# A decoder layer on one core: the second group's expert blocks placed between the first group's, their loads issued earlier, and the last norms on ScalarE

## The chip, the cores and the metric

The kernel runs on one NeuronCore of a Trainium2 chip. The metric is the device time of one execution in microseconds. Time before: 1847.62 us, the median of three runs (1845.48 to 1850.51).

## The reference

A post-norm decoder layer on x of 16 sequences x 256 tokens x 256 channels, all in float32:

```python
x = layernorm(x + attention(x))          # 16 heads, mixes the batch
x = layernorm(x + cross_attention(x, ctx))  # two softmaxes, one subtracted with a gain
x = layernorm(x + ffn(x))                # four experts, the best two of each token
```

The change lies in the last line. The router gives each token logits over four experts; the two best are weighted by a softmax over their two logits. The experts, each from 256 channels to 256:

```python
e0 = silu(x @ sw_w1) * (x @ sw_w3) @ sw_w2                       # "first", 1024 wide
e1 = gelu(((x @ me_eq_w + ..) @ me_wv + ..) @ me_wo .. @ me_c1w + ..) @ me_c2w + ..   # "second", 512 wide
h2 = layer_norm(syn + attn); h2 = layer_norm(h2 + relu(h2 @ ce_f1w + ..) @ ce_f2w + ..)
e2 = h2 @ ce_gen_w + ce_gen_b                                    # "third"
e3 = gelu(x @ ml_w1 + ml_b1) @ ml_w2 + ml_b2                     # "fourth", 1024 wide
out = layernorm(x + rw0 * e[sel0] + rw1 * e[sel1])
```

Constant matrices that follow each other (those of e1, and syn and attn of e2) are multiplied together early in the kernel, so second has one wide product `mw` and third one product `xw` in their place.

## The kernel before

**Tiling.** The 4096 tokens are 32 chunks of 128, four chunks to a pair (512 tokens), eight pairs. The sum x lies in SBUF all the time as `xs`. The two attentions run over the pairs. Each pair, as its cross-attention ends, is routed (`routing`), and its rows are written by GpSimd's indirect DMA into a list in DRAM with one stretch for each expert (`listing`, L404). There are two lists: group 0 holds the tokens of pairs 0 to 6, group 1 those of the last pair. Once the lists are written, each list's lengths are read into registers (`known`), and all later expert work stands under branches on them: a block of an expert has four chunks (512 tokens), and `block` does four chunks, two, or none, by the length.

**A block.** `load` brings 512 list rows into an `xe` buffer (three of them) from SP's queue; `turn` transposes them on TensorE into `xeT` (two buffers), the upper half copied from PSUM by ScalarE, the lower by VectorE (L478). `wide` multiplies with a wide weight into one PSUM bank (8 banks in turn), ScalarE applies GELU, SiLU or ReLU into `hid`; `product` multiplies back to 256 channels, VectorE writes the result into `ye` (one buffer; L504, L506), and SP writes it over the same list rows (L507). `first` comes in two parts (wide, back), `third` in three (product and norm; turn, wide and back product, norm; turn and last product); they are generators, so that the caller places the parts.

**The order.** The instruction order of TensorE, ScalarE and VectorE is the order in which the program writes them down; SP's and GpSimd's queues are laid out by the compiler's scheduler. [...]In the attentions a planner with due times places the work; in the last steps of the cross-attention, at fixed step numbers, `begin` issues the first loads of second in group 0 and `early` places four of its blocks. `turn_tokens` (L1404) turns each finished pair's tokens for the router; for the last two pairs it does so in the `ye` buffer. When the attentions have ended, six weights of the experts are loaded (`sw_w1` to `ml_w2`, L1585), and `rest` does what remains:

1. second's blocks 4 and 5 of group 0, with the first loads of third and first;
2. a loop over third and first of group 0, their parts alternating;
3. fourth's four blocks of group 0; meanwhile `gathers(0)` fetches each token's first expert row from the list by indirect DMA (L628, four for a pair, two slots `ya`), and `add` multiplies it by its weight and adds it to `xs` (L638);
4. group 1: second, third, first and fourth, and between their parts `both`: `add` of the second expert row of one or two pairs and `end`, the layer norm of the pair on VectorE (L140 to L147) and its output DMA.

Blocks beyond the expected lengths (`beyond`) stand under branches that this data does not take.

Of the kernel before, what the change touches and what calls it, by code (L numbers as in the profile page):

```python
# [15 lines left out]
P = 128  # L16
# [54 lines left out]
def decoder_kernel(ctx: ExitStack, tc: tile.TileContext, a: dict, out: bass.AP):  # L71
# [350 lines left out]
    class Experts:  # L422
# [3 lines left out]
        def __init__(self, fe, wb, mw, mb):  # L426
            self.wb, self.mw, self.mb, self.turns = wb, mw, mb, 0
            self.count, self.loaded, self.ready, self.done = {}, [], [], 0
            self.rings = {}
            self.ring(fe, "xe", 3, [P, CPB, D])  # L430
            self.ring(fe, "xeT", 2, [P, 2, TB])
            self.ring(fe, "ye", 1, [P, CPB, D])
            self.ring(fe, "hid1", 1, [P, 4, TB])
# [14 lines left out]
        def known(self, g):  # L448
            self.count[g] = [
                nc.values_load(moe["count"][0:1, g, e:e + 1], min_val=0, max_val=SIZES[g]) for e in range(5)  # L450
            ]
# [14 lines left out]
        def load(self, g, e, i, x=None):  # L466
# [3 lines left out]
            self.loaded.append(x)  # L470

        def turned(self, src, n, t):

            for c in range(2):
# [3 lines left out]
                (DVE.tensor_copy if c else ACT.copy)(t[:, c, :n * P], pt[:, :n * P])  # L478

        def turn(self):  # L480
            t = self.next("xeT")
            self.turned(self.loaded.pop(0), CPB, t)
            self.ready.append(t)
# [25 lines left out]
        def second(self, g, i, sure=False):  # L509
            xT, y, r = self.ready.pop(0), self.next("ye"), self.row(g, 1, i)  # L510
# [11 lines left out]
        def first(self, g, i):  # L522

            xT, r = self.ready.pop(0), self.row(g, 0, i)
# [15 lines left out]
        def fourth(self, g, i, sure=False):  # L540
            xT, y, r = self.ready.pop(0), self.next("ye"), self.row(g, 3, i)
# [11 lines left out]
        def third(self, g, i):  # L553

            xT, r = self.ready.pop(0), self.row(g, 2, i)
# [54 lines left out]
        def begin(self):  # L610
            self.load(0, 1, 0)
            self.load(0, 1, 1)
            self.known(0)
            self.turn()

        def early(self):
            i = self.done
            self.load(0, 1, i + 2)
            self.turn()
            self.second(0, i)  # L620
            self.done += 1


        def gather(self, q, k):
            self.slot = (self.slot + 1) % 2
            t = self.ya[:, self.slot]
# [7 lines left out]
        def add(self):  # L634
            q, k, t = self.gathered.pop(0)
            for n in range(CPB):
                x = xs[:, q * CPB + n, :]
                DVE.scalar_tensor_tensor(x, t[:, n, :], moe["weight"][:, q * CPB + n, k:k + 1], x, ALU.mult, ALU.add)  # L638

        def end(self, q):  # L640
            x = xs[:, q * CPB:(q + 1) * CPB, :]
            layernorm(tiny, x, x)
            SP.dma_start(out=out_v[:, q * CPB:(q + 1) * CPB, :], in_=x)

        def beyond(self, e, i0, i1, work):

            held = self.loaded, self.ready, {k: list(v) for k, v in self.rings.items()}
            with ExitStack() as levels:
                for i in range(i0, i1):
                    levels.enter_context(tc.If(self.count[0][e] > 4 * P * i))  # L650
                    self.loaded, self.ready = [], []
                    self.rings = {k: list(v) for k, v in held[2].items()}
                    self.load(0, e, i)
                    self.turn()
                    work(0, i, True)
            self.loaded, self.ready, self.rings = held

        def rest(self, fl, xw, xb, rb):
# [5 lines left out]
            self.load(0, 2, 0)  # L664
            self.turn()
            self.second(0, 4)
            self.load(0, 0, 0)
            self.turn()
            self.second(0, 5)
            x3 = self.wb.tile([P, CPB, D], F32, tag="cx", name="x3")  # L670
            self.beyond(1, 6, n, self.second)


            with ExitStack() as levels:
                for i in range(n):
                    levels.enter_context(tc.If(self.count[0][4] > 4 * P * i))
                    self.turn()
                    b, c = self.third(0, i), None
                    next(b)
                    if i + 1 < n:  # L680
                        self.load(0, 2, i + 1)
                        self.load(0, 0, i + 1)
                    c = self.first(0, i)
                    next(c)
                    next(b)
                    if i + 1 < n:
                        self.turn()
                    next(c)
                    next(b)
            assert not self.loaded and not self.ready  # L690


            self.ya = self.wb.tile([P, 2, CPB, D], F32, tag="cxp", name="ya")
            self.slot, self.gathered = 0, []
            self.load(0, 3, 0, x3)
            self.load(0, 3, 1)
            self.turn()
            pairs = iter(range(NPAIR - 1))

            def gathers(k, most=2):  # L700
                for q in range(most):
# [4 lines left out]
            gathers(0)  # L706
            ahead = [(0, 3, 2), (0, 3, 3), (1, 1, 0), (1, 2, 0)]
            for i in range(4):
                self.load(*ahead[i])
                if i < 3:  # L710
                    self.turn()
                self.fourth(0, i)
                while self.gathered:
                    self.add()
                gathers(0)
            self.beyond(3, 4, n, self.fourth)
            while self.gathered:
                self.add()


            pairs = iter(range(NPAIR - 1))
            self.known(1)
            gathers(1)
            self.turn()

            def both():
                for q, k, t in list(self.gathered):
                    self.add()
                    if q < NPAIR - 1:
                        self.end(q)  # L730
                gathers(1)

            self.load(1, 0, 0)
            self.turn()
            self.second(1, 0)
            both()
            b = self.third(1, 0)
            self.load(1, 3, 0)
# [851 lines left out]
```

## Time and profile before

| | |
|---|---|
| median of the runs | 1847.62 us |
| profiled execution | 1848.87 us, its span 1846.9 us |
| TensorE busy | 1682.0 us (91%) |
| VectorE busy | 960.4 us (52%) |
| ScalarE busy | 942.6 us (51%) |
| GpSimd busy | 536.5 us (29%) |
| mean granted TensorE clock | 0.958 |
| experts begin (first transposed block) | at 1291.3 us |
| loop over third and first | 1407.7 to 1579.9 us |
| fourth's blocks of group 0 | 1589.6 to 1705.4 us |
| group 1 and the ends | 1705.4 to 1846.9 us; TensorE busy 79 us of it |

The span runs from the first to the last instruction; the execution's own time is some 2 us more. A line of a timeline gives the start, the duration, the engine and line of the kernel, the operation with output and inputs, and in brackets the idle time of the engine before it and what ended that. L119 is the helper of all products, so its rows are told apart by their tiles: `pw` is a wide product, `pr` a product back to 256 channels, `pt` a transposed block. A busy engine is counted by its instructions' durations; waits are not busy.

### The profile page before, as it was taken

To read this page: it belongs to the slowest core of one execution; us is meant where nothing else is said; L and a number is where in the kernel's file an instruction comes from. 1 tells how busy PE (TensorE), PEld (TensorE's weight loads), DVE (VectorE), ACT (ScalarE), POOL (GpSimd) and SP (SyncE) were. 2 spreads that over 40 slices of the span, in tenths; PEclk is the share of its full clock that TensorE was granted. 3 is DMA by queue.
4 is the path that set the end of the run, shared out by engine and by line. 5 is a ranking of instruction groups with operands and counts; after the bars stand their busy time and mean duration, and the time that the engine had idled before them with its cause. 6 is when DMAs were issued, how large, how long until landed. Compare 5 with 4: busy or idle time off the path is not lost. (4 is left out here: it accounts for less than half of the span.)

```text
span 1846.9 us, 32370 instructions
## 1 busy us (share of the span) xinstructions
PE 1682.0 (91%) x12254; PEld 960.4 (52%) x12254; DVE 960.4 (52%) x2033; ACT 942.6 (51%) x1368; POOL 536.5 (29%) x1235
## 2 busy tenths in 40 slices
PE   6999999999999999999999999997987999899743
PEld 2343434343444656656565655564664758566533
DVE  1225656655556876777766666672213334121565
ACT  3547777777777576665655556554322222231210
POOL 5001313212313333344634343445320110131331
PEclk9999999999999999999999999898998999899876
DMA  9912111212112200000101000011333001221322
GB/s 258 297 50 70 65 59 59 69 59 93 58 59 98 65 14 14 3 25 14 37 2 36 2 25 2 25 37 47 102 103 109 20 28 48 82 75 39 106 64 81
DMA packets 117771, 115.34 MB, mean 62 GB/s; under 512 B 7776, under 2 KB 111408, under 8 KB 117584
## 3 DMA queue, kind: packets, MB, share of 16 engines
q1 hardware_dynamic: 108560, 93.08, 15.8%
q0 software_dynamic: 7824, 19.65, 3.6%
q8 instruction: 114, 1.87, 0.4%
q14 instruction: 73, 0.60, 0.1%
q10 hardware_dynamic: 1200, 0.15, 0.1%
HBM read 73.79 MB, written 38.54 MB: 61 GB/s over the span
## 5 line engine op out<-in xcount | busy, mean ns | idle before, releaser
L1307 DVE TENSOR_REDUCE mpad<-p 128x4 f32<-128x1024 f32 x256 | 311.3, 1218 | 142.3 <-PE p L119 141.4
L1313 ACT ACTIVATE e<-p 128x512 f32<-128x512 f32 x512 | 276.7, 596 | 175.5 <-PE p L119 173.7
L841 ACT ACTIVATE h<-ph,L_attn_b 128x1024 f32<-128x1024 f32 x256 | 271.3, 1112 | 160.9 <-PE ph L119 160.9
L119 PE MATMUL p<-qp,kT 32*128 32x256 f32 x2048 | 315.3, 410 | 18.2 <-DVE o L1360 13.3
L119 PE MATMUL p<-kT,qp 32*128 32x256 f32 x2048 | 314.1, 409 | 1.5 <-DVE mpad L1307 1.5
L119 PEld LDWEIGHTS p<-kT,qp 32*128 32x128 f32 x2048 | 193.7, 188 | 91.0 <-issue 49.7
L119 PEld LDWEIGHTS p<-qp,kT 32*128 32x128 f32 x2048 | 207.9, 190 | 31.7 <-issue 25.6
L119 PE MATMUL ph<-qT,w1p 32*128 32x512 f32 x1024 | 152.3, 652 | 3.1 <-ACT h L841 1.8
L935 DVE TENSOR_TENSOR z<-rqb,ra 128x1024 f32<-128x1024 f32 x120 | 151.5, 1265 | 3.7 <-DMA rqb<-rqd 1.7
L119 PE MATMUL pe<-h,w2p 128*32 128x512 f32 x1024 | 138.2, 612 | 1.6 <-DVE enc L858 0.9
L119 PE MATMUL pob<-e,vaug 128*32 128x512 f32 x1024 | 128.3, 620 | 0.0
L942 ACT ACTIVATE z<-z 128x1024 f32<-128x1024 f32 x120 | 127.1, 1060 | 1.3 <-DVE z L935 0.9
L628 POOL DMA_INDIRECT ya<-xlist,place x64 | 62.8, 981 | 205.0 <-DVE xs L638 86.7
L159 POOL TENSOR_SCALAR ln_ve<-ln_mv 128x2 f32<-128x2 f32 x32 | 7.2, 225 | 351.3 <-DVE ln_mv L157 350.5
L119 PE MATMUL pw<-xeT,L_ffn_sw_w 128*128 128x512 f32 (+1 forms) x256 | 85.8, 496 | 12.8 <-DVE xeT L478 12.8
L163 POOL TENSOR_SCALAR xs<-xs,ln_mv,rs_y 128x256 f32<-128x256 f32 x64 | 83.8, 1314 | 3.4
L478 ACT ACT_TABLE_LOAD x17 | 21.8, 1283 | 113.7 <-PE pt L477 113.3
L119 PE MATMUL po<-z,vaug 128*32 128x256 f32 x1024 | 72.8, 389 | 6.7 <-DVE ra L895 1.6
L119 PEld LDWEIGHTS pw<-xeT,L_ffn_sw_w 128*128 128x128 f32 x256 | 50.0, 196 | 47.1 <-issue 28.7
L404 POOL DMA_INDIRECT xlist<-xs,place x64 | 62.7, 980 | 37.1 <-DVE place L401 19.7
L119 PEld LDWEIGHTS ph<-qT,w1p 32*128 32x128 f32 x1024 | 42.5, 184 | 53.8 <-issue 42.0
L1339 ACT COPY ovTb<-pob 128x512 f32<-128x512 f32 x64 | 37.5, 585 | 58.2 <-PE pob L119 58.2
(349 smaller groups left out, 2598.1 us busy)
## 6 DMA issues: line engine op xcount, KB each, us to landing
rqb<-rqd SPq DMA_DIRECT2D x64, 512.0 KB
xlist<-zero SPq DMA_DIRECT2D x16, 1024.0 KB
xe<-xlist SPq DMA_DIRECT2D x21, 512.0 KB
xlist<-ye SPq DMA_DIRECT2D x14, 512.0 KB
xs<-in_x SPq DMA_DIRECT2D x8, 512.0 KB
cx<-in_ctx SPq DMA_DIRECT2D x8, 512.0 KB
qp<-st SPq DMA_DIRECT2D x256, 2.0 KB
out<-xs SPq DMA_DIRECT2D x8, 512.0 KB
```

What stands on the lines that cost most here:

```text
L119: PE.matmul(out=out_, lhsT=lhsT, rhs=rhs, start=start, stop=stop)
L159: POOL.tensor_scalar(ve, mv[:, :, 1], EPS, None, ALU.add)
L163: POOL.tensor_scalar(x, x, mv[:, i, 0:1], r[:, i:i + 1], ALU.subtract, ALU.mult)
L404: put = POOL.indirect_dma_start(xlist[g][:], bass.IndirectOffsetOnAxis(ap=place[:, n, k:k + 1], axis=0), xs[:, q * CPB + n, :], None)
L478: (DVE.tensor_copy if c else ACT.copy)(t[:, c, :n * P], pt[:, :n * P])
L628: POOL.indirect_dma_start(t[:, n, :], None, xlist[group(q)][:], bass.IndirectOffsetOnAxis(ap=moe["place"][:, q * CPB + n, k:k + 1], axis=0),)
L841: ACT.activation(h, phs[gp], AF.Tanh, bias=b1[:, fc:fc + 1])
L935: DVE.tensor_tensor(z, bc(rqbs[u][:, 2 * gp:2 * gp + 2], 2, 2), bc(rk, 3, S), ALU.mult)
L942: ACT.activation(z, z, AF.Exp)
L1307: DVE.tensor_reduce(mpads[j % 2][:, 2 * gp:2 * gp + 2, :, ic], p1, AX.X, ALU.max, negate=True)
L1313: ACT.activation(e[:, gi], p2[gi], AF.Exp)
L1339: ACT.copy(o, po)
```

## The change

It reorders the expert phase. Second's group 0 begins two steps later and its first block three; `turn_tokens` uses `x3`, a buffer now taken at the start, instead of `ye`; `ahead` issues the first loads of third and first before the weights' loads in the program; fourth's first two blocks are loaded before the loop in the program, into `x3` and a slot of `ya`; of group 1, third's three parts and first's two are placed between and after fourth's blocks of group 0; group 1's second and fourth come last, among the ends. A pair's end now does sum and statistics of a chunk in turn, computes the bias `nb` = -mean x r on VectorE and scales and shifts with ScalarE's Identity. The gathers of the second choice have a third slot, `x3`.

```diff
-            if t == 4 * (len(units) + LAG) + 2:
+            if t == 4 * (len(units) + LAG) + 4:
                 ex.begin()
-            if t - 4 * (len(units) + LAG) in (3, 12, 19, 27):
+            if t - 4 * (len(units) + LAG) in (6, 12, 19, 27):
                 ex.early()
         assert planA.ended() and planB.ended()
+        ex.ahead()
...
-                    xTs[q] = late[1].next("ye").rearrange("p c d -> p (c d)").rearrange("p (c t) -> p c t", c=2)
+                    xTs[q] = late[1].x3.rearrange("p c d -> p (c d)").rearrange("p (c t) -> p c t", c=2)
...
+        def ahead(self):
+
+            self.loaded += [self.load(0, 2, 0), self.load(0, 0, 0)]
...
-        def add(self):
+        def add(self, st=None):
             q, k, t = self.gathered.pop(0)
             for n in range(CPB):
                 x = xs[:, q * CPB + n, :]
                 DVE.scalar_tensor_tensor(x, t[:, n, :], moe["weight"][:, q * CPB + n, k:k + 1], x, ALU.mult, ALU.add)
-
-        def end(self, q):
-            x = xs[:, q * CPB:(q + 1) * CPB, :]
-            layernorm(tiny, x, x)
-            SP.dma_start(out=out_v[:, q * CPB:(q + 1) * CPB, :], in_=x)
+                if st is not None:
+                    DVE.bn_stats(st[:, n, :], x)
+            return q
+
+        def end(self):
+
+            st = tiny.tile([P, CPB, 6], F32, tag="ln_st", name="ln_st")
+            mv = tiny.tile([P, CPB, 2], F32, tag="ln_mv", name="ln_mv")
+            q = self.add(st)
+            for c in range(CPB):
+                DVE.bn_aggr(mv[:, c, :], st[:, c, :])
+            ve = tiny.tile([P, CPB], F32, tag="ln_ve", name="ln_ve")
+            DVE.tensor_scalar(ve, mv[:, :, 1], EPS, None, ALU.add)
+            r = rsqrt(tiny, ve, CPB)
+            nb = self.wb.tile([P, 2, CPB], F32, tag="rf", name="ln_nb")[:, 0, :]
+            DVE.scalar_tensor_tensor(nb, mv[:, :, 0], -1.0, r, ALU.mult, ALU.mult)
+            for c in range(CPB):
+                x = xs[:, q * CPB + c, :]
+                ACT.activation(x, x, AF.Identity, bias=nb[:, c:c + 1], scale=r[:, c:c + 1])
+            SP.dma_start(out=out_v[:, q * CPB:(q + 1) * CPB, :], in_=xs[:, q * CPB:(q + 1) * CPB, :])
...
-            self.load(0, 2, 0)
-            self.turn()
-            self.second(0, 4)
-            self.load(0, 0, 0)
-            self.turn()
-            self.second(0, 5)
-            x3 = self.wb.tile([P, CPB, D], F32, tag="cx", name="x3")
+            t5 = self.turn(self.loaded.pop(0))
+            self.second(0, 4, self.ready.pop(0))
+            b_ = self.turn(self.loaded.pop(0))
+            self.second(0, 5, t5)
             self.beyond(1, 6, n, self.second)
 
+            ya = self.wb.tile([P, 2, CPB, D], F32, tag="cxp", name="ya")
+            self.slots, self.gathered = [ya[:, 0], ya[:, 1]], []
+            a_, x0, x1 = self.loaded.pop(0), self.load(0, 3, 0, self.x3), self.load(0, 3, 1, ya[:, 1])
...
-            gathers(0)
-            ahead = [(0, 3, 2), (0, 3, 3), (1, 1, 0), (1, 2, 0)]
-            for i in range(4):
-                self.load(*ahead[i])
-                if i < 3:
-                    self.turn()
-                self.fourth(0, i)
-                while self.gathered:
-                    self.add()
-                gathers(0)
+            self.known(1)
+            x2, y2, x3 = self.load(0, 3, 2), self.load(1, 2, 0), self.load(0, 3, 3)
+            ta, tb = self.rings["xeT"]
+            self.turn(x0, ta)
+            self.turn(x1, tb)
+            gathers(0)
+            self.fourth(0, 0, ta)
+            adds()
+            gathers(0)
+            b = self.third(1, 0, self.turn(y2, ta))
+            next(b)
+            self.turn(x2, ta)
+            y0, y1 = self.load(1, 0, 0), self.load(1, 1, 0)
+            self.fourth(0, 1, tb)
+            adds()
+            gathers(0)
+            next(b)
+            self.turn(x3, tb)
+            y3 = self.load(1, 3, 0)
+            self.fourth(0, 2, ta)
+            adds()
+            gathers(0)
+            next(b)
+            c = self.first(1, 0, self.turn(y0, ta))
+            next(c)
+            self.fourth(0, 3, tb)
+            next(c)
+            adds()
+            self.turn(y1, ta)
+            self.rings["xeT"] = [tb]
             self.beyond(3, 4, n, self.fourth)
...
-            def both():
-                for q, k, t in list(self.gathered):
-                    self.add()
-                    if q < NPAIR - 1:
-                        self.end(q)
-                gathers(1)
-
-            self.load(1, 0, 0)
-            self.turn()
-            self.second(1, 0)
-            both()
-            b = self.third(1, 0)
-            self.load(1, 3, 0)
-            self.turn()
-            next(b)
-            c = self.first(1, 0)
-            next(c)
-            both()
-            next(b)
-            self.turn()
-            next(c)
-            both()
-            next(b)
-            self.gather(NPAIR - 1, 0)
-            self.fourth(1, 0)
-            both()
-            self.gather(NPAIR - 1, 1)
-            both()
-            self.end(NPAIR - 1)
+            self.slots.append(self.x3)
+            last = NPAIR - 1
+            pairs = iter(range(last))
+            gathers(1, 3)
+            self.end()
+            gathers(1, 1)
+            self.second(1, 0, ta)
+            self.turn(y3, tb, copies=(ACT.copy, ACT.copy))
+            self.end()
+            self.gather(last, 0)
+            self.end()
+            gathers(1, 1)
+            self.fourth(1, 0, tb)
+            self.end()
+            gathers(1, 1)
+            self.add()
+            gathers(1, 1)
+            self.end()
+            self.gather(last, 1)
+            for _ in range(3):
+                self.end()
```

The rest of the diff passes the turned block to `first`, `second`, `third` and `fourth` as an argument instead of through a list, and lets `beyond` load into `x3`.

## The prediction

> **What bounds the kernel now.** I read the engine totals first (TensorE is busy 1682.0 of 1846.9 us, everything else about half or less), then TensorE's own timeline of the last stage for the holes and what ended them, then VectorE's, ScalarE's and GpSimd's timelines where a hole ends on them. TensorE's timeline from 1268 us to 1400 us:
>
> ```profile
> 1291.33 1.97 PE L477 MATMUL pt<-ident,xe 128*128 128x128 f32 x8 [7.75 <-DMA xe<-xlist]
> 1350.12 3.64 PE L119 MATMUL pl<-xw,ye 128*128 128x4 f32 x16 [5.11 <-ACT ye L1414]
> 1353.62 1.95 PE L477 MATMUL pt<-ident,xe 128*128 128x128 f32 x8
> ...
> 1397.72 1.94 PE L477 MATMUL pt<-ident,xe 128*128 128x128 f32 x8 [11.84 <-DMA xe<-xlist]
> ```
>
> Columns are start, duration, engine, line, operation, shapes, count, and in brackets the idle time before it with its releaser. Three holes, 24.7 us, two of them waits for a load of list rows. The same view after 1540 us:
>
> ```profile
> 1583.97 1.06 PE L477 MATMUL pt<-ident,x 128*128 128x128 f32 x8 [4.03 <-DVEq L674]
> 1589.62 1.94 PE L477 MATMUL pt<-ident,xe 128*128 128x128 f32 x8 [4.58 <-DMA xe<-xlist]
> 1591.35 15.83 PE L119 MATMUL pw<-xeT,L_ffn_ml_w 128*128 128x512 f32 x32
> ...
> 1691.41 13.98 PE L119 MATMUL pr<-L_ffn_ml_w,hid 128*128 128x256 f32 x64
> 1707.59 3.39 PE L477 MATMUL pt<-ident,xe 128*128 128x128 f32 x16 [2.20 <-DVEq L648]
> ...
> 1740.97 15.83 PE L119 MATMUL pw<-xeT,L_ffn_sw_w 128*128 128x256 f32 x62 [12.84 <-DVE xeT L478]
> ...
> 1775.24 5.40 PE L119 MATMUL pw<-h2T,L_ffn_ce_f1w 128*128 128x256 f32 x14 [16.26 <-DVE h2T L478]
> ```
>
> From 1591 to 1705 us the fourth expert's blocks run without a hole. After 1705.4 TensorE is busy 79 of the remaining 141 us: the second group's experts alternate with VectorE's final sums and norms. One such final sum and norm on VectorE (its timeline, before the last pair):
>
> ```profile
> 1825.93 1.66 DVE L638 SCALAR_TENSOR_TENSOR xs<-ya,weight,xs 128x256 f32<-128x256 f32 x4
> 1827.52 1.40 DVE L140 BATCH_NORM_STATS2 ln_st<-xs 128x6 f32<-128x256 f32 x4
> 1828.83 0.36 DVE L142 BATCH_NORM_AGGREGATE ln_mv<-ln_st 128x2 f32<-128x6 f32 x4
> ...
> 1832.22 1.38 DVE L147 TENSOR_SCALAR xs<-xs,ln_mv,rs_y 128x256 f32<-128x256 f32 x4
> ```
>
> About 7.5 us each, eight of them, in VectorE's order between the copies that TensorE waits for: both engines are bound by the order, neither by its work.
>
> **The sum is made against this execution**, 1848.87 us at a span of 1846.9 (1.97 us around it); the median of the runs is 1847.62, 1.25 under it.
>
> **Start of the experts (-19.7 us).** Two steps' delay of the first load's use puts four transposes (0.60, the row of four) and a product of eight (1.89) into the 7.75 hole: -2.5; the load still comes when the lists are written. The last two pairs' turned tokens go to x3 instead of ye, so ScalarE's copies no longer wait for a write from ye: what stays of the 5.11 hole is a table load (1.28) and the copies' end, about 1.9, and the slow clock after it (transposes 1.95 for 1.07, then 7.50 for 7.03) goes: -4.5. The first loads of third and first now stand on SP's queue around sw_w3, ahead of ce_f2w, sw_w2 and ml_w1, where before they stood behind both ml weights; they wait only for a buffer that a turn some 30 us earlier frees, so the 11.84 hole has no late load left, and its turn costs 1.07 for 1.94: -12.7. Weights move back by one 512 KB load each; sw_w2, the last that matters, is used 60 us after the loop begins. So no cost.
>
> **End of the loop (+5.5).** In SP's queue the load of x0 (fourth's first block) stood early; x3 is now written by the pairs' tokens and by the second expert's extra blocks, and the compiled order puts x0's load behind the loop, and behind ml_w2 (1 MB), which before was issued ahead of the loop. This is the part that works against its purpose. Price: from SP's first issue at 1585.63 to TensorE's start at 1589.62 a 0.5 MB load took 4.0; at 1386.98 two weights and a load (2.5 MB) took 10.7 to 1397.72; so 3.4 per MB, and x0 lands 7.4 after the issue. Then two turns before the first wide product: 1596.9 for 1591.35. Bounds: 0 (the weight is fetched while the jump out of the loop runs) and +14 (x0 shares with 1 MB of gathers and all three other loads). I take 5.5, the two rows' slope.
>
> **Between the fourth's blocks (+37.8 and clock).** Moved in from the tail, at the loop's own two-chunk durations: turn 0.9, third's parts 1.75, 0.6+3.56+3.45, 0.6+2.25, turn 0.9, first's wide part 13.8: 27.8, less one turn of x done earlier: 26.9. New waits: at three boundaries TensorE needs a copy that VectorE issues after the block's results and both pairs' sums. VectorE does this already, hidden behind the next block:
>
> ```profile
> 1619.74 1.72 DVE L506 TENSOR_TENSOR ye<-pr,L_ffn_ml_b_bc 128x256 f32<-128x256 f32 x4 [27.45 <-PE pr L119]
> 1621.37 3.25 DVE L638 SCALAR_TENSOR_TENSOR xs<-ya,weight,xs 128x256 f32<-128x256 f32 x8
> 1624.54 0.68 DVE L478 COPY xeT<-pt 128x512 f32<-128x512 f32 x1
> ```
>
> The block's products end at 1621.0, the copy 4.2 later. Before, that copy was for a block further on; now it is y2's turn (wait 3.4 beyond its transposes), h2T in third's second part (3.4) and in its last part (3.4, and 0.7 for y0's copy). Sum 10.9. The fourth's own blocks have their copies one block ahead, so third's norm (4.8 on VectorE) stays covered. POOL: third's scaling stands behind five gathers that wait for the block's write (begun 4.3 after the block's end, 1.26 apart), done 13.4 after it; TensorE is then in the next block, so no cost.
>
> The Trainium skill (TensorE: Matmul & The Clock Gate, Part 1) says that an idle window of about 3.4 us halves the clock, and about 3.4 us of work restores it: 1.7 for each of my three waits, 5.1. The rows disagree among themselves: after 4.03 us idle the transposes took 1.06 (full), after 2.20 us sixteen took 3.39 where two turns take 2.1. I take 1.0 each, 3.0.
>
> So the fourth's last block ends at 1591.35 - 19.7 + 5.5 + 114.0 + 26.9 + 10.9 + 3.0 = 1732.0 (T) instead of 1705.4.
>
> **Tail (98.0 from T, before 141.5).** The first gather of the second choice starts when the block's write has landed:
>
> ```profile
> 1710.30 0.95 POOL L628 DMA_INDIRECT ya<-xlist,place  x1 [23.54 <-DMA xlist<-ye]
> ```
>
> That is T+4.9; the fourth gather 3.8 later, landing 2.8 after: T+11.5. First's last part (7 on TensorE), its results and y1's turn lie under this. Then the last sum, statistics, 13 small steps of 0.2 and the new bias step: D = T+15.8. One end now costs VectorE 4 x 0.86 (sum and statistic of one chunk alternate, each statistic waiting for its sum: 0.48 + 0.05 + 0.33) + 0.32 + 0.2 + 2.6 + 0.2 = 6.75; 1.38 of scaling goes to ScalarE.
>
> ScalarE's queue is in order, and q0's four scalings stand ahead of the second's GELUs; behind them wait TensorE's product and VectorE's results, and behind those, in VectorE's order, the next end. Two such hand-offs:
>
> - after q0: table load 1.29, four scalings 1.75 (not in the trace; nearest row the 128x256 GELU, 0.47 alone, bounds 1.5 and 2.0), load 1.29, GELU 0.69, product 7.07 and 1.8 for a cold clock (5.40 for 3.3 after the 16.26 hole), results 0.46: D+14.3.
> - q1 and q2, 13.5: D+27.8. Then scalings 1.75 (they share the copies' table), load 1.29, GELU 0.47, product 7.07+1.8, results 0.4: D+40.6. The fourth's wide products were done by D+26, in eight banks.
> - q3 to q7 and one more sum: 33.75 + 1.6: D+76.0. With three slots no gather is late (one set of four is 5.0 and 2.8 to land, against two ends).
> - the last scalings 1.95, and 4.3 from the last result to the end as now: D+82.2.
>
> T + 98.0 = 1830.0 span, 1832.0 for this execution, 1830.7 against the median: **1831**.
>
> On the loads of tables the Trainium skill (ScalarE: Activation LUTs, What ACT_TABLE_LOAD costs) gives 2.66 us for a switch, 1.28 of load and 1.38 of drain; this speaks against norms between GELUs. The row:
>
> ```profile
> 1708.51 1.28 ACT L478 ACT_TABLE_LOAD   x1 [16.15 <-PE pt L477]
> 1709.80 1.07 ACT L478 COPY xeT<-pt 128x512 f32<-128x512 f32 x2
> ```
>
> The copy starts 1.29 after the load. I go by the row; by the rule three switches on the path would add 4.1, 1835.
>
> **Rivals.**
> - *The loop's end swallows the start's gain*: x0's load shares with gathers and loads, +14 for +5.5: 1839. For it: that load waited for nothing before and now stands behind 1 MB. Against: 3.4 per MB.
> - *The hand-offs are hidden* (ScalarE gets q0's norm early and GELUs run while VectorE goes on): the two waits of 14.3 and 12.8 shrink to VectorE's own 2.6 of results and some rest, about -16: 1815. For it: the wide products are done ahead. Against: the queues' order.
> - *Slower*: the alternation of sum and statistic. If each end costs VectorE not 6.75 but over 8.8 (eight ends, 16.6 in all), the tail eats all gain; at 9.5 it is 1853. For it: in the norm's small chain each dependent step takes a full 0.2. Against: in the loop's norms statistic and aggregate alternate at 0.55 a pair.
>
> **How the numbers follow.** A measurement of this kernel tells some 0.3% (5.5 us) from no change. Chances: forecast 0.62 (own range 1821 to 1841), hidden hand-offs 0.15, loop's end 0.14, slower ends 0.09. Under 1842: nearly all of the first (0.60), all of the second, most of the third (0.11): faster 0.86. Within 0.3%: 0.06; slower 0.08. The range that leaves out two in ten: 1815 to 1843.
>
> **What would show it.** Right: no holes of 11.84 and 5.1 before the loop; a hole of some 13 us after it, ended by the load of x; three holes of 3 to 4 us ended by VectorE's copies; in the tail two waits of VectorE of over 10 us for results, ended by TensorE; ends of 6.5 to 7 us. Wrong: a wait in the loop for a weight, ends above 8.8 us, or a tail longer than 115 us after the fourth's last block.

## The result and the profile after

The changed kernel takes **1833.3 us** (median of five runs, 1828.9 to 1835.8); the kernel before, run beside it, 1849.8 us. The ratio is 0.9915 with a 95% interval of 0.9898 to 0.9932, so it is 0.85% faster. The forecast was 1831. The profiled execution has a span of 1828.7 us (its own time 1830.4, mean granted clock 0.957, before 0.958), against a forecast span of 1830.0. One execution of the kernel of experiment 8 took 4051 us where its other three took 1822 to 1825; it counts in no ratio below.

TensorE's timeline of the changed kernel, around the start of the experts; the columns are as in the prediction:

```profile
1289.92 1.97 PE L478 MATMUL pt<-ident,xe 128*128 128x128 f32 x8 [5.63 <-DMA xe<-xlist]
...
1342.06 1.73 PE L119 MATMUL pl<-xw,x 128*128 128x4 f32 x14 [0.41 <-ACT x L1434]
...
1376.16 1.04 PE L478 MATMUL pt<-ident,xe 128*128 128x128 f32 x8
...
1384.82 1.06 PE L478 MATMUL pt<-ident,xe 128*128 128x128 f32 x8 [0.53 <-DVEq L666]
```

The hole of 7.75 us is 5.63 now, that of 5.11 is 0.41, and the turn that had waited 11.84 us (1376.16) waits for nothing. The last row is the loop's first turn: 1384.82, before 1407.66.

The same view from the end of the loop:

```profile
1569.94 1.94 PE L478 MATMUL pt<-ident,x 128*128 128x128 f32 x8 [13.10 <-DMA x<-xlist]
1571.67 1.80 PE L478 MATMUL pt<-ident,ya 128*128 128x128 f32 x8
1573.31 13.90 PE L119 MATMUL pw<-xeT,L_ffn_ml_w 128*128 128x512 f32 x32
...
1603.52 0.67 PE L119 MATMUL pr<-xw,xeT 128*128 128x256 f32 x2 [1.62 <-issue]
1605.30 1.56 PE L119 MATMUL pr<-xw,xeT 128*128 128x256 f32 x6 [1.11 <-DVE xeT L479]
...
1639.30 3.29 PE L119 MATMUL pw<-h2T,L_ffn_ce_f1w 128*128 128x256 f32 x14 [2.63 <-DVE h2T L479]
...
1710.56 13.98 PE L119 MATMUL pr<-L_ffn_ml_w,hid 128*128 128x256 f32 x64
...
1734.28 7.10 PE L119 MATMUL pw<-xeT,mw 128*128 128x512 f32 x16 [1.97 <-DVEq L666]
1748.88 9.75 PE L119 MATMUL pr<-L_ffn_me_c2w,hid 128*128 128x256 f32 x32 [7.49 <-ACT hid L515]
...
1776.77 9.46 PE L119 MATMUL pr<-L_ffn_ml_w,hid 128*128 128x256 f32 x32 [8.46 <-ACT hid L546]
```

The loop's products end at 1556.84, and TensorE then waits 13.10 us for the load of fourth's first block (`x`). From the first wide product, 1573.31, to the end of fourth's last block, 1724.54, third and first of the second group lie between the blocks, with small holes (the largest is the 2.63). The holes of 12.84 and 16.26 us of before are gone; in their place stand 7.49 and 8.46 us ahead of second's and fourth's back products, both ended by ScalarE's `hid`. VectorE's timeline has these two waits as

```profile
1757.37 1.72 DVE L506 TENSOR_TENSOR ye<-pr,L_ffn_me_c2b_bc 128x256 f32<-128x256 f32 x4 [12.65 <-PE pr L119]
...
1765.92 0.48 DVE L641 SCALAR_TENSOR_TENSOR xs<-x,weight,xs 128x256 f32<-128x256 f32 x1
1766.44 0.43 DVE L643 BATCH_NORM_STATS2 ln_st<-xs 128x6 f32<-128x256 f32 x1
...
1772.66 0.16 DVE L657 SCALAR_TENSOR_TENSOR ln_nb<-ln_mv,rs_y 128x4 f32<-128x4 f32 x1
1785.89 0.80 DVE L506 TENSOR_TENSOR ye<-pr,L_ffn_ml_b_bc 128x256 f32<-128x256 f32 x2 [13.07 <-PE pr L119]
```

12.65 and 13.07 us without work. One end, from the first sum at 1765.92 to the bias step's end at 1772.82, takes 6.9 us on VectorE; the one of before in the prediction's rows (1825.93 to 1833.60) takes 7.7.

By stages (starts and ends of the rows above, and of those of before in the prediction):

| stage | before to after, forecast | measured |
|---|---|---|
| up to the loop's first turn | -19.7 | -22.8, of which 1.4 is an earlier first block |
| the loop | 0 | -0.3 |
| loop's end to the first wide product | +5.5 | 16.5 for 11.4: +5.1 |
| first wide product to T, the last block's end | 154.8 | 151.2 |
| T | 1732.0 | 1724.5 |
| T to the end | 98.0 | 104.2 |

T came 7.5 us too early and the tail 6.2 us too long, in opposite directions, so that the span is 1.3 us off.

### The profile page after: what moved, and what is told of

The parts are those of the page before. It is cut to its first block, busy times and chain, and to the rows that moved or that the text cites. A ratio compares the mean times of both kernels' runs of the same rounds, so it can differ in the third digit from the quotient of the medians.

```text
span 1828.7 us, 32380 instructions
## 1 busy us (share of the span) xinstructions
PE 1673.1 (91%) x12254; PEld 954.0 (52%) x12254; DVE 951.4 (52%) x2008; ACT 962.4 (53%) x1404; POOL 537.7 (29%) x1235
## 5 line engine op out<-in xcount | busy, mean ns | idle before, releaser
L1327 DVE TENSOR_REDUCE mpad<-p 128x4 f32<-128x1024 f32 x256 | 311.1, 1217 | 142.7 <-PE p L119 141.5
L631 POOL DMA_INDIRECT ya<-xlist,place x52 | 49.8, 958 | 195.9 <-DVE xs L641 68.5
L404 POOL DMA_INDIRECT xlist<-xs,place x64 | 62.8, 982 | 37.1 <-DVE place L401 19.7
L119 PE MATMUL pr<-L_ffn_ml_w,hid 128*128 128x256 f32 x288 | 65.4, 389 | 8.5 <-ACT hid L546 8.5
```

What stands on the lines that cost most here:

```text
L119: PE.matmul(out=out_, lhsT=lhsT, rhs=rhs, start=start, stop=stop)
L404: put = POOL.indirect_dma_start(xlist[g][:], bass.IndirectOffsetOnAxis(ap=place[:, n, k:k + 1], axis=0), xs[:, q * CPB + n, :], None)
L631: POOL.indirect_dma_start(t[:, n, :], None, xlist[group(q)][:], bass.IndirectOffsetOnAxis(ap=moe["place"][:, q * CPB + n, k:k + 1], axis=0),)
L1327: DVE.tensor_reduce(mpads[j % 2][:, 2 * gp:2 * gp + 2, :, ic], p1, AX.X, ALU.max, negate=True)
```

## The experiments

Each kernel is the changed kernel with the edit named; all of them compute the whole result. A span of a single profile is compared by stages, since the experts' first block starts anywhere from 1288.1 to 1294.1 us in these profiles although no edit lies ahead of it (1289.92 in the changed kernel).

### 1. Third's and first's loads behind the weights again

```diff
-        ex.ahead()
         lefts.close()
...
+        ex.ahead()
         ex.rest(fl, xw, xb, rb)
```

> The first loads of third and first go back behind the six weights in the program; all else as in the changed kernel (profiled span 1828.7). If these loads behind the weights were the 11.84 hole, the hole comes back before the loop (about 12.7 with its slow turn). In this order ml_w2 is issued ahead of the loop again, so the hole after the loop (13.10, ended by the load of x0) should fall by 3.4, the price of 1 MB ahead of it. Sum +9.3: span 1838. Rival, the start's gain is only moved (the loop waits later for a weight): no more than 3 apart from 1828.7. Rival on x0: the hole after the loop stays 13 because jump and gathers set it.

Measured: 1838.7 us, ratio 0.9939 [0.9917, 0.9961], span 1837.7. TensorE's timeline:

```profile
1389.69 1.94 PE L478 MATMUL pt<-ident,xe 128*128 128x128 f32 x8 [11.56 <-DMA xe<-xlist]
...
1577.97 1.94 PE L478 MATMUL pt<-ident,x 128*128 128x128 f32 x8 [5.20 <-SPq L690]
```

The hole ahead of the loop is back at 11.56; with the slow turn and products after it that is 13.7 us (first block to loop's first turn 108.63 for 94.90). So the early loads are what took it away. But the wait behind the loop fell from 13.10 to 5.20, since in this order both `ml_w2` and `x0` are issued ahead of the loop: 7.8 us come back. I had expected only the weight to move. The early loads thus gain 13.7 us at one place and cost 7.8 at another. That the span meets the expected 1838 is luck: this profile also has a first block 1.8 us later and a slower stretch between fourth's blocks, whose row comes back in experiment 6.

### 2 and 3. What ScalarE's scalings hold up

Run 2 scales on VectorE, with sum and statistic still alternating; run 3 leaves the scalings on ScalarE but writes them behind the GELUs (`end(True)` leaves out the scalings and the output's DMA and returns them as a function; the bias then lies in the mean's place, a line not shown here):

```diff
             for c in range(CPB):
                 x = xs[:, q * CPB + c, :]
-                ACT.activation(x, x, AF.Identity, bias=nb[:, c:c + 1], scale=r[:, c:c + 1])
+                DVE.tensor_scalar(x, x, mv[:, c, 0:1], r[:, c:c + 1], ALU.subtract, ALU.mult)
```

> The ends scale on VectorE again (L147's form), sum and statistic still alternate. Theory, the hand-offs in ScalarE's queue cost two waits of VectorE (12.65 and 13.07 in the changed kernel's trace): without scalings ahead of them the GELUs run as soon as the wide products are there, the results of second come 10 earlier and those of fourth 18 earlier; each end costs VectorE 1.2 more, and the last scalings (2.1) no longer follow. Sum -14: span 1815, faster than the changed kernel. Rival, scaling on ScalarE saves what it takes off VectorE: eight ends of 1.2 more, +9: span 1838.

```diff
-            self.end()
+            s0 = self.end(True)
             gathers(1, 1)
             self.second(1, 0, ta)
             self.turn(y3, tb, copies=(ACT.copy, ACT.copy))
-            self.end()
+            s0()
+            s1 = self.end(True)
             self.gather(last, 0)
-            self.end()
+            s2 = self.end(True)
             gathers(1, 1)
             self.fourth(1, 0, tb)
+            s1()
+            s2()
```

> Norms stay on ScalarE, but q0's scalings are written after second's GELUs and the copies of y3, q1's and q2's after fourth's GELUs (the bias lies in the mean's place). Theory: both waits of VectorE fall to about 4 and 6, -18: span 1811. Rival, the GELUs' own time or TensorE's products hold the results: within 3 of 1828.7.

Measured: run 2 1817.5 us, ratio 0.9827 [0.9801, 0.9852], span 1815.9; run 3 **1811.4 us, ratio 0.9798 [0.9771, 0.9824]**, span 1807.8. TensorE's and VectorE's timelines of run 3:

```profile
1742.02 7.07 PE L119 MATMUL pr<-L_ffn_me_c2w,hid 128*128 128x256 f32 x32
...
1758.61 7.07 PE L119 MATMUL pr<-L_ffn_ml_w,hid 128*128 128x256 f32 x32
```

```profile
1747.84 1.72 DVE L506 TENSOR_TENSOR ye<-pr,L_ffn_me_c2b_bc 128x256 f32<-128x256 f32 x4 [2.35 <-PE pr L119]
...
1765.34 0.80 DVE L506 TENSOR_TENSOR ye<-pr,L_ffn_ml_b_bc 128x256 f32<-128x256 f32 x2 [2.14 <-PE pr L119]
```

Both products follow without a hole and at full clock (7.07 for 9.75 and 9.46), and VectorE waits 2.35 and 2.14 for 12.65 and 13.07. T to the end is 82.5 us for 104.2, and 87.9 in run 2. The work on each engine is the same as in the changed kernel; the place of the scalings in ScalarE's order differs (and that of the bias in memory). So the two hand-offs that I had forecast were real, they were the largest cost of the change among those undone here, and ScalarE's scalings as such pay: by the medians they are 6.1 us better than VectorE's when they stand behind the GELUs (5.4 by the stage behind T), and some 16 us worse ahead of them.

### 4. What holds the first gather: the sum

The first gather of the second choices starts at T + 9.2; the forecast was T + 4.9. GpSimd's timeline of the changed kernel names a sum as releaser:

```profile
1733.77 0.95 POOL L631 DMA_INDIRECT ya<-xlist,place  x1 [50.43 <-DVE xs L641]
```

```diff
             self.fourth(0, 3, tb)
-            next(c)
             adds()
+            next(c)
```

> The last pair's first-choice sum (q6) is written ahead of first's last part instead of behind it. Theory: the first gather of the second choice waits for that sum (it starts at 1733.8, 9.2 after the fourth's last block, where the landing of the block's write was predicted at 4.9); moved ahead, it starts at 4.9 and the whole tail moves by 4.3: span 1824.4. Rival, the gather waits for the write (or for first's write): starts at 9 as before, 1828.7.

Measured: 1833.1 us, ratio 0.992 [0.989, 0.9949], span 1826.4 with a first block 1.8 us earlier, so a gain of 0.5. The gather still starts at 9.2 after the block's end (1730.79, the end 1721.55):

```profile
1730.79 0.95 POOL L631 DMA_INDIRECT ya<-xlist,place  x1 [49.59 <-DVEq L666]
```

The theory fell: with the sum out of the way the releaser is VectorE's sequencer at L666, the branch of `beyond` behind fourth's last block.

### 5. What holds the first gather: the branch

```diff
             self.fourth(0, 3, tb)
-            next(c)
             adds()
-            self.turn(y1, ta)
-            self.rings["xeT"] = [tb]
+            hids = self.rings["hid"]
+            self.rings["xeT"], self.rings["hid"] = [tb], hids[1:]
             self.beyond(3, 4, n, self.fourth)
+            self.rings["hid"] = hids
...
             gathers(1, 3)
+            next(c)
+            self.turn(y1, ta)
             self.end()
```

> The second group's last part of first and the turn of y1 are written behind the branch that follows fourth's last block (and behind the three gathers) instead of ahead of it; the additions of q6 ahead of the branch. New theory after e4: the first gather of second choices starts at T + 9.2 and not T + 4.9 because GpSimd passes that branch only when TensorE's and VectorE's part of first, written ahead of it, has been done. Then the gather starts at T + 5 here, the first ends about 4 us sooner, span about 1824.5. Rival: TensorE and VectorE now stop at the branch between fourth's block and first's last part and lose 2 to 4 us there, so the span stays at 1827 to 1830; or the gather stays at T + 9 because it waits for the writes of fourth's results.

Measured: 1828.4 us, ratio 0.9893 [0.9876, 0.9909], span 1827.6. GpSimd's and TensorE's timelines:

```profile
1729.84 0.95 POOL L631 DMA_INDIRECT ya<-xlist,place  x1 [47.32 <-DMA xlist<-ye]
```

```profile
1725.95 8.83 PE L119 MATMUL pr<-L_ffn_sw_w,hid 128*128 128x256 f32 x32 [2.25 <-DVEq L666]
```

The block ends at 1723.71, so the gather starts 6.1 after it and now waits for the write, as it did before the change. So GpSimd had waited for the engines at the branch: part of the new theory holds. But TensorE now stops there for 2.25 us and runs first's last part slowly (8.83 for 7.07), VectorE's copies come later for that and stand ahead of the first end, and that end is done 19.4 after the block for 20.2. The rival is right about the price: 0.8 us gained at the first end, of the 4.3 hoped for.

### 6. Fourth's first block loaded before the loop, and the clock

```diff
-            a_, x0, x1 = self.loaded.pop(0), self.load(0, 3, 0, self.x3), self.load(0, 3, 1, ya[:, 1])
+            a_, x0, x1 = self.loaded.pop(0), self.load(0, 3, 0, ya[:, 0]), self.load(0, 3, 1, ya[:, 1])
```

> Fourth's first block x0 is loaded into the first half of ya, whose place is free before the loop, and no longer into x3; nothing else is changed. My theory says that the 13.1 us hole after the loop is x0's load, queued on SP behind the 1 MB of ml_w2, both written after the loop. With x0 on its way before the loop only x1's and the weights' arrival and the leaving of the loop are left, as before the change: hole 13.1 to about 4 or 5 us, loop's end to the first wide product 16.5 to about 7 to 8 us. Span 1828.7 - 9 = about 1820 us. Rival: TensorE waits for ml_w2 itself or for the queue's arrival, not for x0: the hole moves to the first wide product and the span stays within 3 us of 1828.7.

Measured: 1827.7 us, ratio 0.9882 [0.9866, 0.9899], span 1827.2. TensorE's timeline:

```profile
1563.56 3.65 PE L478 MATMUL pt<-ident,ya 128*128 128x128 f32 x16 [5.01 <-SPq L690]
1567.00 14.35 PE L119 MATMUL pw<-xeT,L_ffn_ml_w 128*128 128x512 f32 x32
...
1636.39 4.85 PE L119 MATMUL pw<-h2T,L_ffn_ce_f1w 128*128 128x256 f32 x14 [2.64 <-DVE h2T L479]
```

The hole fell to 5.01 and the first wide product comes 8.45 after the loop's end for 16.47: 8.0 us gained, as expected. The span is only 1.5 shorter; a first block 1.3 us later hides as much again. Fourth's blocks with what lies between them took 5.5 us longer (from the first wide product to first's last part 156.5 for 151.1), at equal holes (9.4 for 9.2). The row at 1636.39 is one of the places: after a hole of 2.64 the fourteen products take 4.85 us; in the changed kernel, after 2.63, they take 3.29. By stretches of time (columns: stretch, its length, then for each engine busy time and instructions; after these the granted clock, the DMA share and GB/s), of the kernel with the early load and of the changed kernel:

```profile
core 0: us, PE busy (x) PEld busy (x) DVE busy (x) ACT busy (x) POOL busy (x), PEclk, DMA share, GB/s
...
1596.00:1604.00 8.00, 5.26 (x18) 4.21 (x18) 5.30 (x16) 2.21 (x4) 3.33 (x4) 0.66 0.74 234
...
1633.00:1646.00 13.00, 10.31 (x42) 8.38 (x43) 3.33 (x9) 3.78 (x7) 6.52 (x8) 0.87 0.30 93
```

```profile
1601.00:1608.00 7.00, 4.26 (x26) 3.22 (x24) 5.73 (x16) 2.46 (x3) 1.91 (x2) 1.00 0.55 170
...
1636.00:1647.00 11.00, 8.37 (x41) 7.08 (x42) 3.24 (x9) 3.67 (x6) 4.78 (x6) 1.00 0.32 97
```

These are the same boundaries with the same holes (the stretches do not begin and end at the same instruction), at a granted clock of 0.66 and 0.87 in one and 1.00 in the other. Run 1 has the row too, slower still:

```profile
1647.62 6.19 PE L119 MATMUL pw<-h2T,L_ffn_ce_f1w 128*128 128x256 f32 x14 [2.63 <-DVE h2T L479]
```

The next kernel has this edit and one more line, which moves all later holes:

```diff
             self.turn(x0, ta)
+            self.turn(x0, ta)
```

> e5's kernel with the turn of x0 written twice, which puts about 1 to 1.7 us of work ahead of fourth's first block and so moves every later hole against the clock of TensorE. Theory from e5 against the changed kernel (the same holes, but 5.4 us of slower matmuls in e5 only): whether a hole of 1.6 to 2.6 us is followed by slow matmuls depends on when it falls, not on its length; then the matmuls' busy time between the first block and the last part of first goes from 149.8 to some other value between 143 and 150, and if it falls the span is no longer than e5's 1827.2 in spite of more work. Rival: the slow matmuls belong to e5's earlier transfers or order; then busy time stays at 149.8 and the span is 1828 to 1829.

Measured: 1825.7 us, ratio 0.988 [0.9863, 0.9897], span 1824.4, with a first block 1.1 us later than in the kernel without the line. TensorE's timeline at the same place:

```profile
1569.20 13.90 PE L119 MATMUL pw<-xeT,L_ffn_ml_w 128*128 128x512 f32 x32
...
1635.19 3.29 PE L119 MATMUL pw<-h2T,L_ffn_ce_f1w 128*128 128x256 f32 x14 [2.64 <-DVE h2T L479]
```

The hole is 2.64 again, and the products take 3.29. TensorE's rows from the first wide product to first's last part add up to 144.7 us (149.8 without the line, 144.4 in the changed kernel): one more turn, and in the profiles 2.8 us less span. The rival, that the slow products belong to the early load or the order, fell. What is left is when the hole falls: in six kernels with this hole of 2.63 or 2.64 us the fourteen products take 3.29, in the other two 4.85 and 6.19. That the moment decides is inferred, not seen. These are single profiles, the one of the early load is of the slowest of its four executions (1823.2 to 1829.1), and whether the loss comes back in each execution is not shown; between the two kernels' medians the 2.0 us lie within the spread.

### 7. The copies ahead of the sums

```diff
             self.fourth(0, 0, ta)
-            adds()
-            gathers(0)
             b = self.third(1, 0, self.turn(y2, ta))
+            adds()
+            gathers(0)
             next(b)
```

The other two boundaries likewise, with `adds` and `gathers` behind third's part.

> At the three boundaries between fourth's blocks the additions and gathers are written after the turned copy or after third's part, so VectorE makes the copy of turned columns first. My theory: the holes of 1.11, 2.63 and 0.88 us that end on VectorE's copy are VectorE finishing additions first; they go (4.6 us), while the part that ends on ScalarE's copy or the start (1.62, 0.24, 1.57, 1.16) stays, since that is ScalarE's table load and copy. Span 1828.7 - 4.6 = about 1824 us. Rival: the gathers start later by as much, the additions of the last pair end later, and the first gather of the second choices comes as much later: span 1828 to 1830.

Measured: 1823.8 us, ratio 0.9873 [0.9856, 0.989], span 1822.6. TensorE's timeline:

```profile
1603.72 1.97 PE L119 MATMUL pr<-xw,xeT 128*128 128x256 f32 x8 [1.62 <-issue]
...
1635.92 3.29 PE L119 MATMUL pw<-h2T,L_ffn_ce_f1w 128*128 128x256 f32 x14 [0.43 <-DVE h2T L479]
...
1677.53 14.08 PE L119 MATMUL pw<-xeT,L_ffn_sw_w 128*128 128x256 f32 x64 [1.57 <-ACT xeT L479]
```

The holes of 1.11 and 0.88 are gone, 2.63 is 0.43, and 1.16 has become 1.57; the whole of the holes is 5.4 for 9.2 us, first's last part starts 5.4 us sooner, and the tail did not take it back. Of the 5.4, 3.8 are holes; the rest are rows that ran slower in the changed kernel, above all the turn at 1679.83, 1.91 for 1.04 here. The waits for VectorE's copy were waits for the sums ahead of it. What stays is larger: but for the 0.43 it ends with ScalarE's copy, which has a load of its table in front at the first and third boundary and before first's part. At the first, in ScalarE's timeline:

```profile
1601.75 1.28 ACT L479 ACT_TABLE_LOAD   x1 [13.61 <-PE pt L478]
1603.04 0.58 ACT L479 COPY xeT<-pt 128x512 f32<-128x512 f32 x1
```

The copy ends at 1603.62, the product starts at 1603.72.

### 8. Third and first behind all of fourth's blocks

In this kernel the four blocks of fourth follow on each other; behind the branch come `gathers(1, 3)` and then

```python
c = self.first(1, 0, self.turn(y0, tb))
next(b); next(c); next(b)
self.turn(y1, ta)
next(c); next(b)
```

> The second group's third and first are taken from between fourth's blocks and put behind them all, alternating with each other as in the loop, before the ends; fourth's four blocks follow on each other. My theory: the 9.2 us of holes at the boundaries go, and the wait between the last block and the first gathered rows of second choices (T + 9.2 to T + 20) lies under third and first (about 50 us of TensorE), so that the ends find their rows ready. Third's two norms then leave holes on TensorE, covered only by first's two parts. Sum: 9 to 16 us gained, span 1813 to 1820. Rival: third's norms stand open (twice about 7 us in which only first's parts are there) and the ends of the first pairs wait for the same VectorE: span 1826 to 1834.

Measured: 1824.7 us, ratio 0.9868 [0.9848, 0.9887], span 1822.5 with a first block 3.9 us later than in the changed kernel. From the first wide product to the end it takes 1822.5 - 1577.2 = 245.3 us for 255.4, so 10 us less, within the 9 to 16 expected; the late start hides four of them. The holes between the blocks are gone; in their place there is one at the branch:

```profile
1693.59 1.86 PE L478 MATMUL pt<-ident,xe 128*128 128x128 f32 x8 [3.43 <-issue]
```

So in this code third and first cost less behind the blocks, where the gathers run beside them, than between them, where the change puts them. Part of the 10 us is the order of the sums: run 7, between the blocks with the copies first, takes 249.2 for the same stretch.

### 9. The edits together

> The edits of e3 (scalings after the GELUs), e4 (addition first), e5 (x0 early) and e6 (copies first) together. If they add up as spans: 1828.7 - 19.6 (e3, 20.9 less 1.3 of a later start) - 8.0 (e5's shorter wait behind the loop, without the slower matmuls that followed it there) - 6.1 (e6) = about 1795. If the slower matmuls after the holes come with the earlier start as in e5: up to 5 us more, about 1800. Rival: with the blocks ended sooner, VectorE's ends alone set the tail and take part of it back: above 1802.

Measured: 1795.3 us, ratio 0.9719 [0.9702, 0.9736], span 1792.0. The expected span was about 1795; 1.6 of the 3 us under it are an earlier first block. The four edits add up, without the 5 us of slow clock.

The last kernel has the order of 8, the early `x0`, and the ends spread over the second group's work, since all pairs but the last need results of the first group alone (set against the code of 8; only added lines are marked):

```diff
             next(b)
             next(c)
+            s0 = self.end(True)
             next(b)
+            s0()
             self.turn(y1, ta)
+            gathers(1, 1)
             next(c)
             next(b)
+            s1 = self.end(True)
+            gathers(1, 1)
+            s2 = self.end(True)
+            gathers(1, 1)
             self.second(1, 0, ta)
             self.turn(y3, tb, copies=(ACT.copy, ACT.copy))
+            s1()
+            s2()
+            s3 = self.end(True)
...
```

> On e7's order: x0 early; the end of the first pair written inside third and first of the second group, those of the second and third ahead of second, two more ahead of fourth, with the scalings behind the GELUs; third's turned copies both on ScalarE, so that VectorE is free for the ends. Theory: all but the last pair need only the first group's results, whose gathers start right behind the branch, so their ends fit beside the second group's experts, and the end is set by fourth's last results, their gather and the ends of three pairs. From e7's trace: TensorE done about 1769, VectorE then needs about 28 us: 1797, less 8 for x0 and less 4 of e7's late start: span about 1785 (1782 to 1793). Rival: the ends stand in VectorE's queue ahead of first's multiplications, third's sums and the results' additions, and TensorE waits for them: 1800 or more.

Measured: **1784.5 us, ratio 0.965 [0.9634, 0.9666]**, span 1785.2. This is 3.5% under the kernel before and 2.7% under the changed one. TensorE's last products, in its timeline,

```profile
1748.99 7.07 PE L119 MATMUL pr<-L_ffn_ml_w,hid 128*128 128x256 f32 x32
```

follow without a hole and end at 1756.06; in the changed kernel they end at 1786.23. The rival, that the ends hold TensorE up, fell.

## Why the prediction came out right

**The start of the experts** was right in kind and short by 3: the work moved ahead of the first block gave 2.2 for 2.5; the turn of the last pair gave 5.9 for 4.5, since more of the hole went than I left standing (0.41 stays, I had left 1.9 for a table load), though the slow clock behind it did not go as forecast (the wide product takes 8.72, before 7.50, at full speed 7.03); the late load gave 13.3 for 12.7; and 1.4 us are an earlier start. Run 1 shows the cause of the largest part; the other two were not undone and are read from the rows.

**The end of the loop**, +5.5, measured +5.1. The size is right, the reason only in part. I had put the late position of `x0`'s load down to `x3`. Run 1 keeps `x3` and issues that load at 1401.34, ahead of the loop's work, for 1562.24 in the changed kernel: it is `ahead` that pushes it back, and another buffer pulls it forward again (run 6). The rival of +14 fell.

**Between the blocks**, 154.8 forecast, 151.2 measured. This, too, is close because errors cancel. The holes were 9.2 for 10.9, but I had put all of them down to VectorE's sums; run 7 shows 3.8 for that and leaves 5.4, nearly all of it behind ScalarE's copy. The cold clock cost about 1.3 for 3.0: the row with 14 products after the longest hole, 3.29, is at full speed, the four products at 1678.48 and the turn behind them are not (1.56 for 1.13, 1.91 for 1.04). The first wide product took 13.9, where the sum had kept the 15.8 of before. Against these 5.3 us, the work moved in took 28.6 for 26.9, of which 0.9 is a turn that I had taken off although both kernels make it. The clock could have cost more than 5, as run 6 shows with the same holes. The Trainium skill (TensorE: Matmul & The Clock Gate, Part 1) says that the window by which activity is judged runs freely; the kernels of run 6 fit that, but no view here shows the window. The 3.4 us of idle time that the prediction quotes are not needed: the slow rows of runs 1 and 6 follow holes of 2.6. Taking the mean of two rows that disagree was a guess about a phase, and belongs into the range.

**The first gather** is the term that was mis-sized: forecast T + 4.9, measured T + 9.2. It was read from the row of before, where nothing stood between the block and the branch. The change puts first's last part and a turn there, and GpSimd reaches its gathers past that branch only with the others (runs 4 and 5). This moved the first end from T + 15.8 to T + 20.2.

**The hand-offs**: forecast 14.3, 13.5 and 12.8, measured 14.4, 13.7 and 13.9. Four scalings took 2.07 where I took 1.75 within bounds of 1.5 to 2.0. The slow clock took 2.7 and 2.4 (9.75 and 9.46 for 7.07) where I took 1.8; the row I took it from gives 2.1 (5.40 for 3.3). In the last hand-off these two make up 0.9 of the 1.1 missed. In the first they are hidden by a term that was not there: the table load ahead of the scalings ran at 1733.94, under the first end's own work. The loads of tables went by the row, as the rows of ScalarE's timeline show:

```profile
1733.94 1.28 ACT L660 ACT_TABLE_LOAD   x1
1744.75 2.07 ACT L660 ACTIVATE xs<-xs,ln_nb,rs_y 128x256 f32<-128x256 f32 x4 [9.53 <-DVE ln_nb L657]
1746.84 1.28 ACT L515 ACT_TABLE_LOAD   x1
1748.14 2.42 ACT L515 ACTIVATE hid<-pw,mb 128x512 f32<-128x512 f32 x4
```

The second load starts 0.02 after the scalings, and the GELU starts 1.30 after the load's start: not the 2.66 that the Trainium skill (ScalarE: Activation LUTs, What ACT_TABLE_LOAD costs) gives for a switch. The rival of hidden hand-offs is what run 3 makes of the kernel by moving the scalings; its forecast of 1815 lies between runs 2 and 3.

**The ends** took 6.9 us for 6.75, and the five of the tail with one more sum 35.5 for 35.4; the slower rival fell.

TensorE's busy time behind fourth's blocks in the kernel before is 73.6 us of 141.5, not the 79 read there; no term rests on it.

So the total is right because most of the mechanisms were, and its closeness is luck, because two errors cancel: T came 7.5 us early (a better start and full speed at the first wide product) and the tail was 6.2 us long (4.3 for the gather behind the branch, 1.1 in the last hand-off).

## What to carry to other kernels

When a step goes to an engine with an in-order queue, ask what is written behind it there: here the same scalings on ScalarE cost some 16 us more than VectorE's ahead of the GELUs and 6.1 us less behind them. When work is put ahead of a branch, every engine and queue with work behind that branch may wait for it, GpSimd's gathers too; and an earlier load displaces another, so follow the whole queue, not the load alone.

## What the runs showed of the hardware that was not expected

A hole of 2.63 or 2.64 us on TensorE cost nothing in six kernels, 1.56 us of slower products in a seventh and 2.90 in an eighth, with the same instructions around it (3.29, 4.85 and 6.19 us for the fourteen products); in the seventh the sum over fourth's stage was 5.4 us. Of the 8.0 us that a shorter wait gained there, 5.5 were lost again by slower products at holes of the same length.

The experts' first block began at 1288.1 to 1294.1 us in the profiles of the changed kernel and its eleven variants, whose edits all lie behind it. What sets this is open; it is as large as the effects of some of the edits here, and spans of single profiles had to be compared stage by stage.
